# Splitting PSUM into two halves that change use separately, with early scores, VectorE weight factors and later means, in a two-layer attention kernel

## The chip, the cores and the metric

The kernel runs on one core of a Trainium2 chip. The metric is the device time of one execution in microseconds (us); each time quoted is the median of the runs of one submission. Every run of this study was in the fast state. Profiles are of one execution; their span is some 2 us shorter than the measured time. PE is TensorE, DVE is VectorE, ACT is ScalarE, POOL is GpSimd.

## The reference

Two attention layers over a batch of 8 images of 512 channels and 32 x 32 = 1024 positions, all in fp32. Each layer is:

```python
xn  = group_norm(x, 8 groups) * gamma + beta
q, k, v = Wq xn + bq, Wk xn + bk, Wv xn + bv      # 512x512 weights
attn = softmax(q k^T / 8)                          # 8 heads of 64 channels
x   = x + Wp (attn v) + bp
```

So there are 16 jobs (8 images, 2 layers). A job is a linear phase (k, the output projection of the job before, v, q) and an attention phase. The jobs of two images alternate, so that the normalisation of the next job runs during the attention of this one.

## The kernel before

**Linear phases.** Each 512x512 product is done by a Winograd-like scheme: seven products of half size instead of eight, on sums of the blocks of the input (`t`) and of the weights (`S1` to `S4`, the weight factors). A phase has two groups, i = 0 and 1. A group uses four PSUM banks, z, y, u, v:

```python
product(w, src, t, which, i, z, 1, True)      # needs xn only
note(1, z, s1)
product(w, src, t, which, i, y, 2, True)      # needs xn only
join(0, 0, y, s1)
product(w, src, t, which, i, z, 6, False)     # needs the 2nd sum, factor S2
note(2, z, s2)
product(w, src, t, which, i, u, 5, True)      # needs the 1st sum, factor S1
note(5, u, s5)
product(w, src, t, which, i, z, 7, False)     # needs the 3rd sum, factor S3
...                                           # notes and joins, products 3 and 4
```

A note reads PSUM (ACT for k and q), a join adds two parts into the result (DVE).

**Attention phases.** 64 items, each one block of 128 keys for one of 8 groups of queries. Item i does its scores on PE, the exponential on ACT, a running sum of the exponentials on DVE (`acc`; no sum at the first item of a group of eight), and two items later its values on PE. Every fourth item may carry a chore of the next job: statistics, means, scaling, sums.

**PSUM.** One pool of all eight banks, opened anew for each phase; the new pool waits for every user of the pool that it replaces.

```python
with tc.tile_pool(name=f"psa_{n}", bufs=2, space=PSUM) as pool:   # attention: 2 x 2 banks of scores, 2 x 2 of values
...
with tc.tile_pool(name=f"psl_{n}", bufs=2, space=PSUM) as pool:   # linear: z, y, u, v twice
```

The weight factors are made by POOL when weights arrive for the first time; the means (`group_mean`) take a score buffer at items 20 and 24, or at 4 and 8 where the statistics were done earlier.

## Time and profile before

| | before |
|---|---|
| time | 3440.8 us (3437.1 to 3443.2, 4 runs) |
| profile span | 3437.2 us |
| PE busy | 3340.0 us |
| DVE busy | 2318.8 us |
| ACT busy | 1379.5 us |
| POOL busy | 65.6 us |

Busy counts the time in which an engine executes something. The lines that say what bounds the kernel, and where PE loses time, are in the prediction; most of it is lost at the seams, the changes from one phase to the next.

### The profile page before, as it was taken

The numbers are of one execution on the slowest core, as the hardware profiler recorded it, in microseconds if no ns is written. First come the engines' busy times: TensorE is split into PE (matmuls) and PEld (weight loads), VectorE is DVE, ScalarE is ACT, GpSimd is POOL, SyncE is SP. The second block draws the span as 40 slices with busy tenths as digits, with TensorE's granted clock in tenths as the row PEclk, the third lists the DMA queues.
The fourth block names the chain that finished last, engine by engine and source line by source line (L and its number), as shares of the span: only waits on it lengthen the run. The fifth ranks groups of instructions, "written<-read, shape, count | busy, mean of one in ns | idle before, by whom it ended". The sixth has DMA issues, their size and how long they took to land.

```text
span 3437.2 us, 50762 instructions
## 1 busy us (share of the span) xinstructions
PE 3340.0 (97%) x20996; PEld 1487.2 (43%) x20996; DVE 2318.8 (67%) x3160; ACT 1379.5 (40%) x1535; POOL 65.6 (2%) x58
## 2 busy tenths in 40 slices
PE   7999999999999999999999999999999999999999
PEld 4335353353533535344353443534435354353533
DVE  4775948659386584865839668485683956748566
ACT  1532616335163351623516245162451625416153
POOL 3001000000000000000000000000000000000000
PEclk9999999999999999999999999999999999999999
DMA  5011010120201100021010010002101001000101
GB/s 190 14 48 71 22 37 15 54 77 22 73 15 35 47 24 22 15 70 61 23 71 18 32 50 21 22 18 81 51 21 71 18 32 50 21 22 21 44 11 43
DMA packets 79534, 141.81 MB, mean 41 GB/s; under 512 B 37568, under 2 KB 45760, under 8 KB 75200
## 3 DMA queue, kind: packets, MB, share of 16 engines
q1 hardware_dynamic: 79296, 138.50, 11.7%
q8 instruction: 166, 2.72, 0.3%
q14 instruction: 72, 0.59, 0.1%
HBM read 104.35 MB, written 31.98 MB: 40 GB/s over the span
## 4 chain that ended last, share of the span: by engine, by line
PE 86%; DVE 10%; issue 2%; ACT 2%; DMA 0%; SPq 0%; DVEq 0%; POOL 0%; ACTq 0%; POOLq 0%
PE sc L426 21%; PE po L449 19%; PE z L264 14%; PE u L264 9%; DVE acc L437 5%; PE z L257 5%; PE y L264 5%; PE v L264 5%; PE u L257 3%; ACT e L431 2%; PE y L257 2%; PE v L257 2%; PE pp L398 1%; DVE q L469 1%; DVE acc L435 1%
## 5 line engine op out<-in xcount | busy, mean ns | idle before, releaser
L431 ACT ACTIVATE e<-sc 128x1024 f32<-128x1024 f32 x1024 | 1046.5, 1024 | 674.7 <-PE sc L426 613.4
L426 PE MATMUL sc<-q,k 64*64 64x512 f32 x8192 | 1063.8, 591 | 34.7 <-DVE q L309 14.0
L449 PE MATMUL po<-e,v 64*64 64x512 f32 x8192 | 1057.3, 589 | 0.0
L437 DVE TENSOR_TENSOR acc<-acc,e 128x1024 f32<-128x1024 f32 x768 | 938.3, 1222 | 76.5 <-ACT e L431 25.1
L426 PEld LDWEIGHTS sc<-q,k 64*64 64x64 f32 x8192 | 307.8, 133 | 597.3 <-issue 540.6
L449 PEld LDWEIGHTS po<-e,v 64*64 64x64 f32 x8192 | 313.3, 133 | 565.6 <-issue 554.3
L264 PE MATMUL z<-xn,w 128*128 128x512 f32 x512 | 248.9, 610 | 41.4 <-DVE q L469 35.7
L305 ACT ACTIVATE sa<-z,vec_sb 128x512 f32<-128x512 f32 x128 | 88.0, 687 | 487.9 <-PE z L264 487.9
L435 DVE TENSOR_TENSOR acc<-e,e 128x1024 f32<-128x1024 f32 x128 | 156.4, 1222 | 137.4 <-ACT e L431 136.3
L264 PEld LDWEIGHTS z<-xn,w 128*128 128x128 f32 x512 | 97.0, 192 | 164.0 <-issue 107.3
L459 DVE TRANSPOSE_TENSOR_REDUCE r<-acc 128x32 f32<-128x1024 f32 x128 | 158.5, 1238 | 0.6
L362 ACT ACTIVATE sb<-z,vec_sb 128x512 f32<-128x512 f32 x30 | 20.6, 687 | 340.9 <-PE z L264 340.9
L334 ACT COPY sb<-u 128x512 f32<-128x512 f32 x32 | 18.8, 586 | 337.5 <-PE u L257 337.5
L264 PE MATMUL y<-xn,w 128*128 128x512 f32 x256 | 124.9, 611 | 0.0
L264 PE MATMUL z<-t,w 128*128 128x512 f32 x256 | 122.0, 599 | 2.1 <-DVE t L239 2.1
L257 PE MATMUL z<-w,xn 128*128 128x256 f32 x512 | 121.0, 379 | 0.0
L264 PE MATMUL u<-t,w 128*128 128x512 f32 x256 | 120.4, 592 | 0.0
L264 PE MATMUL u<-xn,w 128*128 128x512 f32 x256 | 120.3, 592 | 0.0
L264 PE MATMUL v<-t,w 128*128 128x512 f32 x256 | 120.3, 592 | 0.0
L309 DVE TENSOR_TENSOR q<-sb 128x512 f32<-128x512 f32 x32 | 22.4, 700 | 142.1 <-ACT sb L305 142.1
L264 PE MATMUL z<-q,w 128*128 128x512 f32 x240 | 112.8, 592 | 0.0
L257 PEld LDWEIGHTS z<-w,xn 128*128 128x128 f32 x512 | 97.3, 190 | 20.1 <-issue 7.7
(106 smaller groups left out, 2731.3 us busy)
## 6 DMA issues: line engine op xcount, KB each, us to landing
w<-keep SPq DMA_DIRECT2D x24, 1792.0 KB, 7.2
rb<-rd SPq DMA_DIRECT2D x256, 128.0 KB, 2.9
x<-x_dram SPq DMA_DIRECT2D x32, 512.0 KB, 5.8
out_dram<-x SPq DMA_DIRECT2D x64, 256.0 KB, 2.0
keep<-w SPq DMA_DIRECT2D x8, 1792.0 KB, 5.7
lr<-r SPq DMA_DIRECT2D x512, 4.0 KB, 1.7
w<-wqkv_dram SPq DMA_DIRECT2D x24, 256.0 KB, 5.2
w<-wp_dram SPq DMA_DIRECT2D x8, 256.0 KB, 5.9
```

What stands on the lines that cost most here:

```text
L257: nc.tensor.matmul(ps[:, ti * CH : (ti + 1) * CH], block[:, cc, t0 : t0 + P], w[:, slot, cc, :], start=(first and ti == 0 and cc == 0), st ...
L264: nc.tensor.matmul(ps, w[:, slot, cc, i * P : (i + 1) * P], block[:, cc, :], start=(first and cc == 0), stop=(cc == 1), skip_group_check=True,
L305: nc.scalar.activation(out, ps, AF.Identity, bias=env.vec(layer, bias, oc))
L309: nc.vector.tensor_add(dst[:, 2 * oh + i, cols], a, b)
L398: nc.tensor.matmul(ps, w[:, cc, oc * P : (oc + 1) * P], qt[0][:, cc, cols], start=(cc == 0), stop=(cc == NC - 1),)
L426: nc.tensor.matmul(sc[h * HD : (h + 1) * HD, j, :], k[r, hp, k0 : k0 + HD], q[r, hp, sh * HALF : (sh + 1) * HALF], start=True, stop=True,)
L431: nc.scalar.activation(e, sc, AF.Exp, scale=SCALE)
L435: nc.vector.tensor_add(acc[g], es[i - 1], e)
L437: nc.vector.tensor_add(acc[g], acc[g], e)
L449: nc.tensor.matmul(po[g][j * HD : (j + 1) * HD, h, :], v[r, kc, d0 : d0 + HD], e[r, j, :], start=(kc == 0), stop=(kc == NT - 1),)
L459: nc.vector.tensor_reduce(r, a.rearrange("p j (b e) -> p (j b) e", e=RP), AX.X, ALU.add, apply_transpose=True,)
L469: nc.vector.tensor_add(q[:, hp, cols], p[:, 1, :], px)
```

## The change

Its intent: keep PE busy over the seams between phases. PSUM becomes two halves (scores or z, y, u, v of group 0 in one; values or group 1 in the other), each turned over when its own users are done. The first two scores of an attention phase are issued inside the last q products. The weight factors go to DVE. The means move to items 24 and 32, and what follows them later too. Cut to its core:

```diff
-        with tc.tile_pool(name=f"psa_{n}", bufs=2, space=PSUM) as pool:
-        with tc.tile_pool(name=f"psl_{n}", bufs=2, space=PSUM) as pool:
+    def banks(half, use):
+        if half in ps:
+            ps.pop(half)[0].__exit__(None, None, None)
+        turns[0] += 1
+        guard = tc.tile_pool(
+            name=f"ps{half}_{turns[0]}", bufs=2 if use == "two" else 1, space=PSUM,
+            side=("left", "right")[half], reuse_waits="tile",
+        )
+        ps[half] = (guard, guard.__enter__())
 ...
-        nc.gpsimd.tensor_add(w[:, S1], w[:, S3], w[:, A22])      # and three more
+        def factor(part):                                        # called later, piece by piece
+            if part == 0:
+                nc.vector.tensor_add(w[:, S1], w[:, S3], w[:, A22])
 ...
         product(w, src, t, which, i, y, 2, True)
         join(0, 0, y, s1)
+        yield                          # the first k phase runs two groups side by side
         product(w, src, t, which, i, z, 6, False)
 ...
         join(1, 1, s3, s5)
+        if break_in is not None:
+            break_in()                 # scores 0 and 1, in q's second group
         product(w, src, t, which, i, u, 3, False)
 ...
+        if together:                   # first k phase only
+            b = channel_group(n, K, BK, kt[0], 1)
+            next(a)
+            next(b)
+            for step in together:      # sums of xn, factors of k
+                step()
+            run(a)
+            run(b)
 ...
-            chores = reads + steps                               # one at each fourth item
+            chores = dict(zip((4, 8, 12, 16), reads))
+            chores.update(zip((24, 32, 36, 40, 44, 48, 52), steps))
+            chores.update({56: t[0], 60: t[1]})
```

A thing that the title of the change doesn't say: the new pools are also opened with `reuse_waits="tile"`. A tile then waits only for the last users of its own banks, not for all users of the pool that lay there.

More of the change, by code (lines that the diff above doesn't have):

```diff
@@ L1 @@
-from contextlib import ExitStack, contextmanager
+from contextlib import ExitStack
 import concourse.bass as bass
@@ L82, in fast_path @@
     wdram = ctx.enter_context(tc.tile_pool(name="wdram", bufs=1, space=DRAM))
-    ps = {}
+    ps, turns = {}, [0]
     bv_sb = [acts.tile([P, C], F32, name=f"bv_sb{i}") for i in range(2)]
@@ L104, in advance, with bank @@
             t[1]()
-    @contextmanager
-    def attention_banks(n):
-        with tc.tile_pool(name=f"psa_{n}", bufs=2, space=PSUM) as pool:
-            ps["pool"] = pool
-            yield
-    @contextmanager
-    def linear_banks(n):
-        with tc.tile_pool(name=f"psl_{n}", bufs=2, space=PSUM) as pool:
-            ps["pool"] = pool
-            yield
+    def banks(half, use):
[7 more added lines that the diff above has]
+        ps[half] = (guard, guard.__enter__())
     def two_banks(tag, name):
-        return ps["pool"].tile([P, 2, HALF], F32, tag=tag, name=name)
-    def bank(tag, name):
-        return ps["pool"].tile([P, HALF], F32, tag=tag, name=name)
+        return ps[0 if tag == "sc" else 1][1].tile([P, 2, HALF], F32, tag=tag, name=name)
+    def bank(half, tag, name):
+        return ps[half][1].tile([P, HALF], F32, tag=tag, name=name)
     weights = {}
@@ L139, in fetch @@
         if weights.get(which, (None, None))[0] == layer:
-            return
-        w = wpool.tile([P, NW, 2, CH], F32, tag=f"w{which}", name=f"w_{which}_{layer}_{len(stored)}_{clock[0]:.0f}")
+            return None
+        turns[0] += 1
+        w = wpool.tile([P, NW, 2, CH], F32, tag=f"w{which}", name=f"w_{which}_{turns[0]}")
         weights[which] = (layer, w)
@@ L144, in fetch, with factor_later @@
             nc.sync.dma_start(w, stored[which, layer])
-            return
+            return None
         for at, i, j in ((A11, 0, 0), (A12, 0, 1), (A22, 1, 1), (S3, 1, 0)):
             nc.sync.dma_start(w[:, at], raw_block(layer, which, i, j))
-        nc.gpsimd.tensor_add(w[:, S1], w[:, S3], w[:, A22])
-        nc.gpsimd.tensor_sub(w[:, S2], w[:, S1], w[:, A11])
-        nc.gpsimd.tensor_sub(w[:, S3], w[:, A11], w[:, S3])
-        nc.gpsimd.tensor_sub(w[:, S4], w[:, A12], w[:, S2])
         keep = wdram.tile([P, NW, 2, CH], F32, name=f"keep_{which}_{layer}")
         stored[which, layer] = keep
-        later(60.0, lambda: nc.sync.dma_start(keep, w))
+        def factor(part):
+            if part == 0:
+                nc.vector.tensor_add(w[:, S1], w[:, S3], w[:, A22])
+            elif part == 1:
+                nc.vector.tensor_sub(w[:, S2], w[:, S1], w[:, A11])
+            elif part == 2:
+                nc.vector.tensor_sub(w[:, S3], w[:, A11], w[:, S3])
+            else:
+                nc.vector.tensor_sub(w[:, S4], w[:, A12], w[:, S2])
+                later(1.0, lambda: nc.sync.dma_start(keep, w))
+        return factor
+    def factor_later(delay, factor):
+        if factor is not None:
+            for part in range(4):
+                later(delay + 1.7 * part, lambda part=part: factor(part))
     def load_x(b):
@@ L181, in group_mean @@
             if alone:
-                pm = bank("z", name)
+                pm = bank(0, "z", name)
                 nc.tensor.matmul(pm[:, :NC], env.blk, src, start=True, stop=True)
@@ L229, in fast_path @@
     qt, kt, vt = [None], [None], [None]
-    background = []
     def combine(src, t, part):
@@ L245, in product @@
     def product(w, src, t, which, i, ps, p, first):
-        slot, block = {
-            1: (A11, src[:, 0:2, :HALF]), 2: (A12, src[:, 2:4, :HALF]),
-            3: (S4, src[:, 2:4, HALF:]), 4: (A22, t[:, 2]), 5: (S1, t[:, 0]),
-            6: (S2, t[:, 1]), 7: (S3, src[:, 0:2, HALF:]),
-        }[p]
+        slot = (A11, A12, S4, A22, S1, S2, S3)[p - 1]
+        if p in (4, 5, 6):
+            block = t[0][:, {5: 0, 6: 1, 4: 2}[p]]
+        else:
+            rows = 0 if p in (1, 7) else 2
+            cols = slice(0, HALF) if p in (1, 2) else slice(HALF, S)
+            block = src[:, rows : rows + 2, cols]
         if which == V:
@@ L268, in product, with seven @@
         advance(1.72)
-    def seven(n, which, src, t, i, note, join):
+    def seven(n, which, src, t, i, note, join, break_in=None):
         w = weights[which][1]
         tag = f"{which}_{n}_{i}"
-        z, y = bank("z", f"z{tag}"), bank("y", f"y{tag}")
-        u, v = bank("u", f"u{tag}"), bank("v", f"v{tag}")
+        z, y, u, v = (bank(i, f"{b}", f"{b}{tag}") for b in "zyuv")
         sa = epool.tile([P, 2, HALF], F32, tag="e", name=f"sa{tag}")
@@ L294, in seven @@
         join(1, 0, v, s3)
-    def channel_phase(n, which, bias, dst):
-        layer = jobs[n][1]
-        for i in range(2):
-            def note(k, ps, out):
-                if k == 5:
-                    nc.scalar.copy(out, ps)
-                else:
-                    oc = i if k < 3 else 2 + i
-                    nc.scalar.activation(out, ps, AF.Identity, bias=env.vec(layer, bias, oc))
-            def join(oh, sh, a, b):
-                cols = slice(sh * HALF, (sh + 1) * HALF)
-                nc.vector.tensor_add(dst[:, 2 * oh + i, cols], a, b)
-            seven(n, which, xn[0], tx[0], i, note, join)
-            if background:
-                background.pop(0)()
@@ L315, in k_phase, with run, channel_group, note @@
-    def k_phase(n):
-        kt[0] = acts.tile([P, NC, S], F32, tag="k", name=f"k_{n}")
-        channel_phase(n, K, BK, kt[0])
-    def q_phase(n):
-        qt[0] = acts.tile([P, NC, S], F32, tag="q", name=f"q_{n}")
-        channel_phase(n, Q, BQ, qt[0])
+    def run(*parts):
+        parts = list(parts)
+        while parts:
+            parts = [g for g in parts if next(g, g) is not g]
+    def channel_group(n, which, bias, dst, i, break_in=None):
+        layer = jobs[n][1]
+        def note(k, ps, out):
+            if k == 5:
+                nc.scalar.copy(out, ps)
+            else:
+                oc = i if k < 3 else 2 + i
+                nc.scalar.activation(out, ps, AF.Identity, bias=env.vec(layer, bias, oc))
+        def join(oh, sh, a, b):
+            cols = slice(sh * HALF, (sh + 1) * HALF)
+            nc.vector.tensor_add(dst[:, 2 * oh + i, cols], a, b)
+        return seven(n, which, xn[0], tx, i, note, join, break_in)
@@ new lines, in k_phase, with q_phase, first_scores @@
+    def k_phase(n, together=()):
+        kt[0] = acts.tile([P, NC, S], F32, tag="k", name=f"k_{n}")
+        a = channel_group(n, K, BK, kt[0], 0)
+        if together:
[6 more added lines that the diff above has]
+            run(b)
+        else:
+            run(a)
+            banks(1, "one")
+            run(channel_group(n, K, BK, kt[0], 1))
+    def q_phase(n, reads):
+        qt[0] = acts.tile([P, NC, S], F32, tag="q", name=f"q_{n}")
+        run(channel_group(n, Q, BQ, qt[0], 0))
+        for step in reads:
+            step()
+        banks(0, "two")
+        att = Attention(n)
+        def first_scores():
+            att.scores(0)
+            att.scores(1)
+        run(channel_group(n, Q, BQ, qt[0], 1, first_scores))
+        banks(1, "two")
+        return att
@@ L346, in join @@
                 )
-            seven(n, V, xn[0], tx[0], i, note, join)
+            run(seven(n, V, xn[0], tx, i, note, join))
     def proj_phase(n):
@@ L375, in join, with plain_weights @@
                     nc.sync.dma_start(out[b, oc * P : (oc + 1) * P, cols], at(oh, sh))
-            seven(n, O, qt[0], to[0], i, note, join)
+            run(seven(n, O, qt[0], to, i, note, join))
         if layer == 1 and b + 2 < B:
             load_x(b + 2)
-    def last_proj(n):
-        b, layer = jobs[n]
-        xt = xs[b]
+    def plain_weights(n):
+        layer = jobs[n][1]
         w = wpool.tile([P, NC, C], F32, tag=f"w{K}", name="w_last")
@@ L387, in last_proj, with plain_proj @@
         return w
-    def last_proj_run(n, w):
+    def plain_proj(n, w):
         b, layer = jobs[n]
         xt = xs[b]
-        tags = "zyuv"
         for sh in range(2):
@@ L395, in last_proj_run @@
             for oc in range(NC):
-                ps = bank(tags[oc], f"pp_{n}_{sh}_{oc}")
+                ps = bank(sh, "zyuv"[oc], f"pp_{n}_{sh}_{oc}")
                 for cc in range(NC):
@@ L406, in last_proj_run, with __init__, scores @@
                 advance(3.5)
-    def attention(n, chores):
-        q, k, v = qt[0], kt[0], vt[0]
-        last = n + 1 == len(jobs)
-        if last:
-            groups = [(hp, sh) for sh in range(2) for hp in range(HP)]
-        else:
-            groups = [(hp, sh) for hp in range(HP) for sh in range(2)]
-        steps = [(g, kc) for g in range(len(groups)) for kc in range(NT)]
-        es, acc, po = {}, {}, {}
-        def scores(i):
+    class Attention:
+        def __init__(self, n):
+            self.n, self.q, self.k, self.v = n, qt[0], kt[0], vt[0]
+            if n + 1 == len(jobs):
+                self.groups = [(hp, sh) for sh in range(2) for hp in range(HP)]
+            else:
+                self.groups = [(hp, sh) for hp in range(HP) for sh in range(2)]
+            self.steps = [(g, kc) for g in range(len(self.groups)) for kc in range(NT)]
+            self.es, self.acc, self.po = {}, {}, {}
+        def scores(self, i):
+            n, q, k = self.n, self.q, self.k
+            groups, steps, es, acc = self.groups, self.steps, self.es, self.acc
             g, kc = steps[i]
@@ L437, in scores, with values @@
                 nc.vector.tensor_add(acc[g], acc[g], e)
-        def values(i):
+        def values(self, i):
+            n, v = self.n, self.v
+            groups, steps, es, po = self.groups, self.steps, self.es, self.po
             g, kc = steps[i]
@@ L452, in values, with finish @@
                     )
-        def finish(g):
+        def finish(self, g):
+            n, q = self.n, self.q
+            groups, acc, po = self.groups, self.acc, self.po
             hp, sh = groups[g]
@@ L493, in finish, with run @@
             later(11.5 if ends else 14.6, normalise)
-        for i in range(len(steps) + LEAD):
-            if i < len(steps):
-                scores(i)
-            if i >= LEAD:
-                values(i - LEAD)
+        def run(self, chores):
+            steps = self.steps
+            for i in range(2, len(steps) + LEAD):
+                if i < len(steps):
+                    self.scores(i)
+                self.values(i - LEAD)
                 g, kc = steps[i - LEAD]
                 if kc == NT - 1:
-                    finish(g)
+                    self.finish(g)
                     advance(0.85)
-            if chores and i >= 4 and i % 4 == 0:
-                chores.pop(0)()
-            advance(1.71)
-        assert not chores
+                if i in chores:
+                    chores[i]()
+                advance(1.71)
     def judge():
@@ L527, in fresh_to, with fetch_bv, sums, start @@
         to[0] = acts.tile([P, 3, 2, HALF], F32, tag="v", name=f"to_{n}")
+    def fetch_bv(layer):
+        nc.sync.dma_start(bv_sb[layer], bv[layer : layer + 1, :].to_broadcast([P, C]))
+    def sums(n):
+        def start():
+            tx[0] = acts.tile([P, 3, 2, HALF], F32, tag="t", name=f"t_{n}")
+            combine(xn[0], tx[0], 0)
+        return [start] + [lambda part=part: combine(xn[0], tx[0], part) for part in (1, 2, 3)]
+    def out_sums(n, src):
+        def start():
+            to[0] = acts.tile([P, 3, 2, HALF], F32, tag="v", name=f"to_{n}")
+            combine(src, to[0], 0)
+        later(12.6, start)
+        for part in range(1, 4):
+            later(12.6 + part * 1.7, lambda part=part: combine(src, to[0], part))
+    banks(0, "one")
+    banks(1, "one")
     load_x(0)
-    fetch(K, 0)
-    fetch(V, 0)
+    factor_k = fetch(K, 0)
+    factor_v = fetch(V, 0)
     fetch_bv(0)
-    fetch(Q, 0)
+    factor_q = fetch(Q, 0)
     load_x(1)
-    fetch(O, 0)
+    factor_o = fetch(O, 0)
     fetch_bv(1)
-    with linear_banks(0):
-        reads, steps = norm_steps(0, alone=True)
-        for step in reads + steps:
-            step()
-        fresh_t(0)
-        for part in range(4):
-            combine(xn[0], tx[0], part)
-        k_phase(0)
-        v_phase(0)
-        q_phase(0)
+    reads, steps = norm_steps(0, alone=True)
+    for step in reads + steps:
+        step()
+    t = sums(0)
+    k_phase(0, [
+        t[0], t[1], lambda: factor_k(0), lambda: factor_k(1), t[2], lambda: factor_k(2),
+        lambda: factor_k(3), t[3], lambda: factor_later(1.0, factor_v),
+    ])
+    factor_later(1.0, factor_q)
+    v_phase(0)
+    factor_later(1.0, factor_o)
+    att = q_phase(0, [])
     reads, steps = norm_steps(1)
@@ L549, in fast_path @@
         last = n + 1 == len(jobs)
+        chores = {}
         if last:
-            w = last_proj(n)
-            chores = []
-        else:
-            chores = reads + steps
-            chores += [lambda: (fresh_t(n + 1), combine(xn[0], tx[0], 0))]
-            chores += [lambda: combine(xn[0], tx[0], 1)]
-        with attention_banks(n):
-            attention(n, chores)
-        with linear_banks(n + 1):
-            if last:
-                advance(100.0)
-                advance(100.0)
-                judge()
-                last_proj_run(n, w)
-                continue
-            src = qt[0]
-            combine(xn[0], tx[0], 2)
-            combine(xn[0], tx[0], 3)
-            later(12.6, lambda: (fresh_to(n), combine(src, to[0], 0)))
-            for part in range(1, 4):
-                later(12.6 + part * 1.7, lambda part=part: combine(src, to[0], part))
-            k_phase(n + 1)
-            layer2 = jobs[n + 2][1] if n + 2 < len(jobs) else None
-            if layer2 is not None:
-                fetch(K, layer2)
-            proj_phase(n)
-            if n + 2 < len(jobs):
-                fetch(O, jobs[n + 1][1])
-            v_phase(n + 1)
-            if layer2 is not None:
-                fetch(V, layer2)
-                reads, steps = norm_steps(n + 2)
-                if layer2 == 1:
-                    background.append(lambda r=tuple(reads): [f() for f in r])
-                    reads = []
-            q_phase(n + 1)
-            if layer2 is not None:
-                fetch(Q, layer2)
@@ new lines, in fast_path @@
+            w = plain_weights(n)
+        else:
+            t = sums(n + 1)
+            chores = dict(zip((4, 8, 12, 16), reads))
+            chores.update(zip((24, 32, 36, 40, 44, 48, 52), steps))
+            chores.update({56: t[0], 60: t[1]})
+        att.run(chores)
+        banks(0, "one")
+        if last:
+            banks(1, "one")
+            advance(100.0)
+            advance(100.0)
+            judge()
+            plain_proj(n, w)
+            break
+        t[2]()
+        t[3]()
@@ new lines, in fast_path @@
+        out_sums(n, qt[0])
+        ahead = n + 2 < len(jobs)
+        k_phase(n + 1)
+        if ahead:
+            factor_later(8.0, fetch(K, jobs[n + 2][1]))
+        proj_phase(n)
+        if ahead:
+            factor_later(8.0, fetch(O, jobs[n + 1][1]))
+        v_phase(n + 1)
+        reads = steps = []
+        if ahead:
+            factor_later(8.0, fetch(V, jobs[n + 2][1]))
+            reads, steps = norm_steps(n + 2)
+        early = ahead and jobs[n + 2][1] == 1
+        att = q_phase(n + 1, reads if early else [])
@@ L591, in general_path @@
+        if early:
+            reads = []
+        if ahead:
+            factor_later(125.0, fetch(Q, jobs[n + 2][1]))
+    for half in (1, 0):
+        ps.pop(half)[0].__exit__(None, None, None)
 @with_exitstack
```

## The prediction

> **What bounds the kernel now.** I read the page first, for the engine that sets the time.
>
> ```profile
> PE 3340.0 (97%) x20996; PEld 1487.2 (43%) x20996; DVE 2318.8 (67%) x3160; ACT 1379.5 (40%) x1535; POOL 65.6 (2%) x58
> ...
> PEclk9999999999999999999999999999999999999999
> ```
>
> TensorE is busy for 3340.0 of 3437.2 us. No scheduling change can shorten those; it can win back only the 97 us of idle, and slow matmuls. So the second view was the waits of PE alone (who released it, us in total, times, longest):
>
> ```profile
> PE z L264 <- DVE q L469: 35.7, 15, 2.7
> PE sc L426 <- DVE q L309: 14.0, 16, 0.9
> PE sc L426 <- ACT e L431: 11.8, 46, 0.3
> PE pm L183 <- DVE mv L178: 10.6, 1, 10.6
> PE sc L426 <- DVE mean L193: 8.9, 8, 1.2
> PE z L264 <- ACT xn L213: 5.7, 1, 5.7
> PE pp L398 <- DVE q L469: 2.4, 1, 2.4
> PE z L264 <- DVE t L239: 2.1, 1, 2.1
> ```
>
> The counts name the places: 15 and 16 are the seams between the 16 attention and 16 linear phases, 8 is one item in two, 1 is the start or the end. A "busy" PE need not run at peak, so the third view was the timeline of PE at one seam of each kind (start, duration, engine, line, count, idle before):
>
> ```profile
> 634.08 2.75 PE L449 MATMUL po<-e,v 64*64 64x512 f32 x24
> 639.19 1.98 PE L264 MATMUL z<-xn,w 128*128 128x512 f32 x4 [2.35 <-DVE q L469]
> 641.01 1.88 PE L264 MATMUL y<-xn,w 128*128 128x512 f32 x4
> ...
> 733.85 1.88 PE L264 MATMUL v<-t,w 128*128 128x512 f32 x4
> 736.60 1.95 PE L426 MATMUL sc<-q,k 64*64 64x512 f32 x16 [0.88 <-DVE q L309]
> 738.88 1.09 PE L426 MATMUL sc<-q,k 64*64 64x512 f32 x8 [0.32 <-ACT e L431]
> 739.78 1.04 PE L449 MATMUL po<-e,v 64*64 64x512 f32 x8
> 740.64 1.04 PE L426 MATMUL sc<-q,k 64*64 64x512 f32 x8
> ```
>
> In steady state a product (four matmuls) starts every 1.717 us (0.429 each, against a shown duration of 0.592, whose tail overlaps the next one), and an attention step of 16 quarter-array matmuls also takes 1.717. The last values are six rounds of four at once, so the next matmul could start at 634.08 + 6 x 0.429 = 636.65; the first seam loses 639.19 - 636.65 = 2.54 us, and another 0.10 in its first weight load. At the second the first score should start at 733.85 + 1.717 = 735.57, and the fourth at 739.00 after three scores and one value group of 0.86 each; it starts at 740.64, so 1.64 us are lost.
>
> A fourth view, the first linear products after an attention phase, shows a loss that no wait counts:
>
> ```profile
> 213.80 3.01 PE L264 MATMUL z<-xn,w 128*128 128x512 f32 x4 [2.35 <-DVE q L469]
> ...
> 216.60 2.59 PE L264 MATMUL y<-xn,w 128*128 128x512 f32 x4
> ```
>
> From 213.80 the first two products take 5.23 us until the third starts, against 3.54 after 639.19. Five of the 15 seams and the last projection look so: weight loads follow each other by 0.85 us, half speed. About 1.6 us each.
>
> [...] The kernel before changes mode only across waits, so its trace can't show the cost; [...] the 128x1024 sum of xn at 22.08 us took 2.29 us beside GpSimd's factors and 1.22 elsewhere, and so did their GpSimd partner (1.26 alone, 2.24 beside it).
>
> **The change, part by part.** The work on PE stays the same.
>
> Attention to linear. Before, the linear pool could not open until the whole attention pool was read, the last reader being the final add of the values (L469). Now k's first group uses the half of the scores, free since the last exponential (210.0 in job 0, before PE ends its values at 211.3). Its first two products need nothing new. The third and fourth need sums made in attention; the fifth needs the third sum, due 6.9 us into the phase, while VectorE made it 4.1 us after PE ended its values; moving the first two sums to items 56 and 60 adds perhaps 1 us of backlog, still in time. Saved: 16 x 2.54 (15 seams and the last projection) [...]: 38.1 us.
>
> Linear to attention. The first two scores run inside the last q products, in the half that group 0 of q has left. Their exponentials take 2 x 1.02 us on ACT under two products of 1.72, so the third score and the first values find all they need. Saved 16 x 1.64 = 26.2; but three mode changes per seam (to quarter, back, to quarter: 0.21 + 0.27 + 0.21 = 0.69) cost 11.0. Net 15.2 us.
>
> Half-speed products: with no idle, six times 1.6 us go: 9.6.
>
> Means at items 24 and 32. In attention VectorE is nearly full: per group of 8 steps (13.7 us) seven sums of 1.22, a reduction 1.25, the value add 0.65, the inversion 1.2, the scaling 0.67 come to 12.3, and with the statistics (5.9) it lags. The score buffer taken by the mean is given back late:
>
> ```profile
> 775.15 1.09 PE L426 MATMUL sc<-q,k 64*64 64x512 f32 x8 [1.19 <-DVE mean L193]
> ```
>
> At an item whose step has no sum (24 and 32 start groups) VectorE reaches the copy a sum of 1.22 us sooner, and has had four more steps to catch up. I take 8 of the 8.9 us.
>
> Start. [...]
>
> ```profile
> 14.04 1.22 DVE L205 TENSOR_TENSOR mul<-var,vec_sb 128x4 f32<-128x4 f32 x1 [1.20 <-POOL var L201]
> 15.29 6.87 DVE L207 TENSOR_SCALAR xn<-x,mean,mul 128x1024 f32<-128x1024 f32 x4
> ...
> 18.36 3.78 PE L264 MATMUL z<-xn,w 128*128 128x512 f32 x4 [5.72 <-ACT xn L213]
> ```
>
> The small multiply would take 0.16 and the first scaling 0.81 (the mean later is 0.81, here 1.72), so PE starts about 2.0 us sooner. The interleaving of the two k groups gives four products that need no sums, which covers the 2.1 us wait for t. From 18.36 to 98.33 the 42 products (72.3) lost 7.7 us; about 1 of that is the seam, 2.1 the wait, most of the rest half speed[...]: 2 more. Start: 6 us.
>
> GpSimd beside later phases: the second attention phase has sums of 1.74 and 2.10 us instead of 1.22, with about 1 us lost on PE. Saved: 1. Against it, 32 factor operations of 0.69 us (22 us, from the 128x512 adds) go to VectorE, mostly in linear phases, where it is busy 40 to 47 of 97 us: beside PE. But VectorE is in order: a factor that waits for its weights (four transfers, 5.2 us to landing, issued after the phase's last product; the factor is placed some 8.6 us later) holds the v and proj evictions that PE needs next. For three such phases I charge 2 us.
>
> Sum: 38.1 + 15.2 + 9.6 + 8 + 6 + 1 - 2 = 75.9, so 3440.8 - 75.9 = 3365. From below: 658 products of 1.717, 224 v products of 1.727, 1024 steps of 1.717, 64 last matmuls of 0.429 and 15 x 0.93 us of means are 3316; with 16.4 before the first product, 2.8 of half speed, 13.6 of mode changes, 5.2 after PE's last and about 2.5 between profile span and measured time: 3357, with nothing for small waits. I say 3362.
>
> **The rivals.** (a) Mode changes cost more [...] At 0.5 us each instead of 0.24 the 64 of them take 16 us more: 3378, within 2%. (b) VectorE becomes the bound at the seams: it is busy 104 of 116 us in an attention phase with statistics, and now PE no longer pauses to let it catch up 4 us per item. Against it: ACT, not VectorE, feeds k and q, and the exponentials wait for VectorE only 0.7 us at most now. If k's fifth product waited 2 us at each seam, 30 us would go back: 3393. (c) The whole gain arrives and mode changes hide in the pipeline: 3349. (d) The idle of a seam was only a buffer wait over a true one, so that it comes back under another name: against it, every operand of the first products is ready at 211. I give it little.
>
> **Range and chances.** 2% is 3372. The centre, 3362, is 10 us under it; (a) and a mild (b) lie across the line, (c) on the far side. Range 3348 to 3382. Faster by over 2%: 0.75; within 2%: 0.23; slower: 0.02, for nothing adds work to PE but mode changes.
>
> **What would show it.** The waits of PE on q L469 and on the last q add gone, and the mean's wait at most 1 us in all; PE idle below 35 us; a period of 207 to 209 us from item to item (211.45 at best before); the first matmuls after a seam at 0.43 spacing, those of a mode change later by about 0.2; the first product near 16.4. Wrong if mode changes leave 0.5 us holes, if k's fifth product waits on the sum of xn, or if v and proj products wait on VectorE behind a factor.

How it priced the mode changes: the 0.21 and 0.27 us in its sum of 0.69 are the author's estimate from the trace of the kernel before. The shown duration of a matmul exceeds the spacing by 0.592 - 0.429 = 0.16 us, and the first loads after idle cost 0.05 (quarter tiles) or 0.10 us (full ones). The 38.1 us for the first seam are 16 x 2.54 less 16 x 0.16.

## The result, and the profile after

The changed kernel takes 3362.4 us (3361.3 to 3363.9, 4 runs) against 3440.8: 78 us less. The ratio is 0.977 (95% interval 0.976 to 0.979). Ratios here are the mean time of one kernel's fast runs over that of the other's of the same rounds, so not quite the ratio of the medians quoted.

The same two lines of the page, now of the changed kernel:

```profile
PE 3328.4 (99%) x20996; PEld 1483.2 (44%) x20996; DVE 2319.4 (69%) x3192; ACT 1378.3 (41%) x1535; POOL 16.9 (1%) x26
...
PEclk9999999999999999999999999999999999999999
```

PE has the same 20996 matmuls; its idle time went from 97.2 to 32.3 us (3360.7 - 3328.4). The waits of PE alone:

```profile
PE pm L195 <- DVE mv L190: 11.2, 1, 11.2
PE sc L470 <- ACT e L475: 6.6, 30, 0.2
PE z L277 <- DVE w L155: 4.7, 1, 4.7
PE z L277 <- ACT xn L225: 3.6, 1, 3.6
PE pvar L195 <- DVE dev L208: 0.8, 1, 0.8
```

The groups with counts of 15 and 16, the seams, are gone, and so are the waits on the mean. What is left is the start, and 30 short waits at the means. One line is new: 4.7 us on a weight factor (`w`). The two seams, in PE's timeline of the changed kernel (a mode change is PE's switch between matmuls on the whole 128x128 array and four 64x64 ones at once):

```profile
207.40 2.76 PE L495 MATMUL po<-e,v 64*64 64x512 f32 x24
210.09 1.98 PE L277 MATMUL z<-xn,w 128*128 128x512 f32 x4
...
93.43 1.88 PE L277 MATMUL z<-xn,w 128*128 128x512 f32 x4
95.24 1.95 PE L470 MATMUL sc<-q,k 64*64 64x512 f32 x16
97.11 1.98 PE L277 MATMUL u<-xn,w 128*128 128x512 f32 x4
98.94 1.88 PE L277 MATMUL v<-t,w 128*128 128x512 f32 x4
100.75 1.09 PE L470 MATMUL sc<-q,k 64*64 64x512 f32 x8
```

From attention to linear: the six rounds of values end their slots at 207.40 + 2.57 = 209.97, and k starts at 210.09; 0.11 us are lost where 2.54 were, besides the 0.10 in the first loads that both kernels have. From linear to attention, 93.43 plus three products and two scores' worth twice (4 x 1.717) gives 100.30 for the third score; it starts at 100.75 and its own first loads cost 0.05: 0.50 us lost where 1.64 were. From job to job (the prediction says from item to item) the period is now 207.9 us, once 208.2 (in the chain of work, the last values of successive phases start at 207.58, 415.47, 623.36 and so on), where it was 211.5 to 215. At all 64 mode changes after the start the first load begins together with the first matmul, where most tiles in steady state have theirs 0.43 us ahead.

Now the start, in the timeline of DVE and PE together:

```profile
24.46 1.88 PE L277 MATMUL y<-xn,w 128*128 128x512 f32 x4
26.44 0.69 DVE L330 TENSOR_TENSOR k<-y,sa 128x512 f32<-128x512 f32 x1 [2.74 <-PE y L277]
27.05 1.22 DVE L248 TENSOR_TENSOR t<-xn 128x1024 f32<-128x1024 f32 x1
...
31.00 3.75 PE L277 MATMUL z<-t,w 128*128 128x512 f32 x4 [4.67 <-DVE w L155]
```

DVE stands idle for 2.74 us until PE has finished the fourth product, only to add two parts of k (the join), and makes the sum `t` after that. PE then waits 4.7 us for the sums and factors and runs its next products at half speed (a duration of 3.75 for four matmuls instead of 1.88; the mean granted clock is 0.62 from 31.00 to 36.64), and the gain of the start is lost: the last q product before attention would, without the scores between, start at 98.94 - 2.08 = 96.86 us (2.08 = two scores 1.72 and one pair of mode changes 0.36), against 95.58 in the kernel before. About 0.6 of these 1.3 us is scatter: PE's first matmul, which waits for the statistics of the first image, came at 11.20 in this execution and at 10.64 in that of the kernel before.

### The profile page after: what moved, and what is told of

Its sections match the earlier page's. It is cut to its first block, busy times and chain, and to the rows that moved or that the text cites. A ratio compares the mean times of both kernels' runs of the same rounds, so it can differ in the third digit from the quotient of the medians.

```text
span 3360.7 us, 50799 instructions
## 1 busy us (share of the span) xinstructions
PE 3328.4 (99%) x20996; PEld 1483.2 (44%) x20996; DVE 2319.4 (69%) x3192; ACT 1378.3 (41%) x1535; POOL 16.9 (1%) x26
## 4 chain that ended last, share of the span: by engine, by line
PE 97%; ACT 1%; DVE 1%; DMA 0%; issue 0%; SPq 0%; POOL 0%; DVEq 0%; POOLq 0%
PE sc L470 26%; PE po L495 25%; PE z L277 15%; PE u L277 10%; PE z L270 5%; PE y L277 5%; PE v L277 5%; PE u L270 3%; PE y L270 2%; PE v L270 2%; ACT e L475 1%; PE pp L440 1%; DVE acc L481 0%; DMA x<-x_dram 0%; DVE stats L189 0%
## 5 line engine op out<-in xcount | busy, mean ns | idle before, releaser
L537 DVE TENSOR_TENSOR q<-q,rb 128x512 f32<-128x512 f32 x128 | 86.6, 677 | 40.8 <-DMA rb<-rd 40.8
```

What stands on the lines that cost most here:

```text
L537: nc.vector.tensor_mul(q[:, hp, cols], q[:, hp, cols], rb)
```

## The experiments

The theory after reading the two traces: the seams give the gain, by freeing banks earlier; the place of the means gives some 10 us; the start loses about 7 us to the order of work in DVE's queue. What was open: whether the halves, the finer waits or the early scores win the seams, what a mode change costs, whether the means' gain comes from "later" or from the place, and what the factors' move is worth. Twelve kernels ran; all gave correct results. They ran in four submissions, and the kernel before ran again in each: its medians were 3439.5 to 3440.9 us, so that differences of 2 or 3 us between submissions are known to about 1 us.

**1. Sums first at the start.** In the first k phase the joins move behind the sums and factors in DVE's queue:

```diff
         product(w, src, t, which, i, y, 2, True)
-        join(0, 0, y, s1)
         yield
+        join(0, 0, y, s1)
```

> The changed kernel with one edit: in the first k phase VectorE makes the sums of xn and k's weight factors before the two joins of k, not after them. Theory: the changed kernel lost its gain at the start because the joins, which wait for TensorE's second and fourth product (at 22.7 and 26.2 us), stand ahead of the sums in VectorE's queue, so the fifth product waited 4.7 us (31.0 instead of 26.2) and then ran at half speed. With the edit PE has no wait between its first product (16.8 us) and the first attention phase, the fifth product starts at about 26.2 us, the eighth-in-line full-speed start at 36.6 moves to about 29.6, and the span falls by 7 us (3360.7 to about 3354; ratio to before 0.975). Rival: the sums wait for the scaling and shifting of xn or for the weights' transfers, and the fifth product starts no sooner than 29 us; the span falls by less than 3 us.

Measured: 3355.1 us (ratio 0.975), 7.4 us less than the changed kernel; span 3352.4. The first product began at 16.29 (0.55 of that gain is the scatter of the statistics again), and the fifth product no longer waits; DVE's second factor is done 3.2 us before:

```profile
21.25 0.69 DVE L155 TENSOR_TENSOR w<-w 128x512 f32<-128x512 f32 x1
...
25.16 1.88 PE L277 MATMUL z<-t,w 128*128 128x512 f32 x4
```

The theory holds: an order of instructions, not any data, cost 7 us.

**2. k in the other half.** k's first group takes the half that the values leave last, its second the half of the scores:

```diff
-        a = channel_group(n, K, BK, kt[0], 0)
+        a = channel_group(n, K, BK, kt[0], 0, None, 0 if together else 1)   # its half
 ...
-            banks(1, "one")
-            run(channel_group(n, K, BK, kt[0], 1))
+            banks(0, "one")
+            run(channel_group(n, K, BK, kt[0], 1, None, 0))
 ...
-        banks(0, "one")                                  # after attention
+        banks(1, "one")
```

> The changed kernel with k's first group put in the half of PSUM that the values' sums leave last, and its second in the half of the scores; everything else in two halves as now. Theory: the first k product waits again for the last add of the values. That add now ends 6.2 us after the last round of values starts (213.59 - 207.40; before 5.05), so the wait is 3.5 us at 15 seams, 52 us, plus half speed at some of the seams or all (1.6 us each, 8 to 24 us): span 3420 to 3437, the gain of the change mostly gone. Rival: a wait behind the buffer would have come anyway and little (under 15 us) changes.

Measured: 3361.4 us (ratio 0.977), no change. The theory fell as stated. The halves were not what freed k: within the values' half, z and y fall on the buffer of the group of queries before the last one, which has long been read, and the pool's finer waits see that. So the halves and the finer waits had to be told apart:

**3 and 4. Finer waits alone, and halves alone.** The kernel before with `reuse_waits="tile"` added to its two pools and nothing else; and the changed kernel with `reuse_waits="tile"` taken out:

```diff
-        with tc.tile_pool(name=f"psa_{n}", bufs=2, space=PSUM) as pool:
+        with tc.tile_pool(name=f"psa_{n}", bufs=2, space=PSUM, reuse_waits="tile") as pool:
 ...                                                      # and psl_ likewise
```

> The kernel before with one edit: its two alternating pools of all eight banks stay, but a tile that lands on banks of the pool that was closed waits only for the last users of its own banks, as the changed kernel's pools do, and not for every user of the closed pool. No halves, no early scores, factors on GpSimd, means as before. It asks whether the halves or the finer waits win the seams, after the run with k in the other half moved nothing. Theory (finer waits): at the first seam z, y and u fall on banks of the scores and of the values' free buffer, so the 2.54 us less 0.11 for the mode change go 16 times (39 us) and six half-speed stretches (9.6 us); at the second the last add of q is not waited for, 0.88 us become 0.09, 16 times (13 us); the third score's 0.6 us and the means' 8.9 us stay. Span 3437 - 61 = 3376, time about 3380. Rival (the halves are needed): within 10 us of before.

> The changed kernel with its halves, but each pool waits for all users of the pool that lay there. Theory: the halves alone also suffice, since k's first group and the first two scores fall on a half that is long free; only the first values of a phase must wait for the last add of q in their half (due about 0.1 us after they are now issued) and v's later groups change nothing, so 0 to 3 us are lost: 3362 to 3366. Rival: the halves do nothing without the finer waits, and 40 us or more come back.

Measured: the finer waits alone 3374.5 us (ratio 0.981), the halves alone 3362.5 (ratio 0.977, as the changed kernel). In the first, the seam is closed by the words in the pool alone:

```profile
208.02 2.75 PE L449 MATMUL po<-e,v 64*64 64x512 f32 x24
210.71 1.98 PE L264 MATMUL z<-xn,w 128*128 128x512 f32 x4
```

210.71 is again 0.11 us after the end of the slot at 208.02 + 2.57. The finer waits alone gave 65 us, where I expected 60. Either suffices for this seam; the change has both.

**5. Neither.** k in the other half and pools that wait for all users:

> Both taken away at the first seam: k's first group in the values' half and pools that wait for all users of the one before. Theory: now k's first product does wait for the last add of the values, about 3.5 us at 15 seams (52 us), and half of the seams or more then run 1.6 us slow: span 3415 to 3437. If it moves nothing either, the add was never what k waited for.

Measured: 3433.9 us (20 runs, 3430.1 to 3439.1; ratio 0.998): the whole gain of the change gone. The wait is the one named, in PE's list and in the timeline of the first seam:

```profile
PE z L277 <- DVE q L518: 53.4, 15, 4.1
...
214.28 3.78 PE L277 MATMUL z<-xn,w 128*128 128x512 f32 x4 [3.50 <-DVE q L518]
```

The duration of 3.78 is half speed: the next product starts 3.58 us later, at 217.86, where 1.717 is the steady period. In the chain of work, ten of the 15 seams begin with such slow products, with gaps of 3.6 us in the mean of all 15 (53.4 / 15) and 4.1 at most; in the kernel before, with 2.4 us in the mean (35.7 / 15), it was five. So the gap between the values' last add and k was a wait for a buffer and for nothing else.

**6. No early scores.** The two scores after the last q product:

```diff
-        run(channel_group(n, Q, BQ, qt[0], 1, first_scores))
+        run(channel_group(n, Q, BQ, qt[0], 1))
+        first_scores()
```

> The changed kernel with the first two scores issued after the last q product instead of between its products. Theory: most of the 1.64 us per seam came back through the two halves (the scores no longer wait for the last add of q, 0.9 us and its restart), and only a wait of the third score on the first exponential (0.6 us by the trace of before) is what the break-in itself removes, while it costs two more mode changes that the trace shows at 0.09 to 0.2 us each. So without it the seam loses about 0.7 us where it now loses 0.5: span +3 us, up to 3364. Rival: the break-in is what wins the seam; without it 1.3 us per seam or more come back: +20 us, 3381.

Measured: 3364.9 us (ratio 0.978), 2.5 us slower than the changed kernel. What comes back is the third score's wait on the first exponential (PE's list: 46 waits of 12.0 us instead of 30 of 6.6); the period from job to job is 208.10 instead of 207.89. The theory holds: of the 18 us won at this seam, the early scores won 2 or 3.

**7. Early scores apart.** One score before each of the last two q products, so two more mode changes per seam:

> The changed kernel with the two early scores apart: one before the last but one q product, one before the last. That adds two mode changes per seam, 32 in all, and no other work; it measures what a mode change costs. Theory (0.09 to the quarter array with 0.05 in its first loads, 0.10 back with 0.11): 0.36 us per seam more, 5.7 us in all, span 3366. My prediction's estimate (0.48 per pair): 7.7 us, 3368. Rival (a change costs 0.5 us, hidden here by something): 16 us.

Measured: 3367.1 us (ratio 0.979), 4.6 us more. The first product of that execution began 0.7 us sooner than in the changed kernel's (the statistics were done at 10.5 instead of 11.2), so the 16 extra pairs cost about 5.3 us, 0.33 each. In the timeline they cost 0.36, and the period from job to job, which has no start in it, is 0.36 longer too (208.25 instead of 207.89):

```profile
94.43 1.09 PE L473 MATMUL sc<-q,k 64*64 64x512 f32 x8
95.45 1.98 PE L277 MATMUL u<-xn,w 128*128 128x512 f32 x4
97.37 1.09 PE L473 MATMUL sc<-q,k 64*64 64x512 f32 x8
```

From 94.43 to 95.45 are 1.02 us for 0.86 of scores, from 95.45 to 97.37 1.92 for a product of 1.717. That is 0.09 to the quarter array and 0.05 in its first loads, 0.11 back and 0.11 in the first loads. The estimate of 0.48 was a third too high; the rival of 0.5 per change is out.

**8 and 9. The place of the means.** At items 20 and 24 as before (with the scalings, and the sums at 48 and 52, back where they were), and at 23 and 31:

```diff
-            chores.update(zip((24, 32, 36, 40, 44, 48, 52), steps))
+            chores.update(zip((20, 24, 28, 32, 36, 40, 44), steps))      # run 8
+            chores.update(zip((23, 31, 36, 40, 44, 48, 52), steps))      # run 9
```

> The changed kernel with the means at items 20 and 24 and what follows them four to eight items sooner, as in the kernel before. Theory: the score that takes the mean's buffer next waits 1.2 us or a little more at the 8 or so items whose statistics lie in attention, since VectorE no longer has a pause at the seams: +9 to +13 us, 3371 to 3375, with the wait on the mean back in PE's list. Rival (the waits came from the pauses and are gone with them): +0 to +3.

> The changed kernel with the two means at items 23 and 31 instead of 24 and 32, everything else where it is. Between 20 and 24 both the time that VectorE has to catch up and the place in the group change: item 24 starts a group and has no sum, item 23 ends one and has one of 1.22 us that stands ahead of the mean's copy. Theory (the place counts): at 23 the slack falls by 1.22 us; about 0.5 to 1 us is waited for at some 8 to 15 first means, +4 to +12 us, 3366 to 3374. Rival (only being later counts): within 2 us of 3362.

Measured: 3377.9 us (ratio 0.982) and 3383.8 us (ratio 0.983): 15.5 and 21.4 us more than the changed kernel, both more than I expected. PE's waits, first of the run at 20 and 24, then of the run at 23 and 31:

```profile
PE sc L470 <- DVE mean L205: 12.6, 15, 1.2
```

```profile
PE sc L470 <- DVE mean L205: 9.2, 15, 1.7
...
PE sc L470 <- DVE var L212: 6.0, 15, 0.7
```

Each place waits at 15 jobs, not 8: in these runs every job has its means there, where the kernel before had half of them at items 4 and 8. And the list is short of the truth: the shown end of a matmul lies 0.16 us after the next one could start (0.592 shown, 0.429 apart), so by that overlap each listed wait costs 0.16 more: 12.6 + 15 x 0.16 = 15.0, and 9.2 + 6.0 + 30 x 0.16 = 20.0, near the measured 15.5 and 21.4. (By the period from job to job the surplus is 0.23 a wait in these two runs: 209.31 or 208.64 us at item 20, for listed waits of 1.19 or 0.53, against 207.89. The slower first loads after idle, 0.05, are part of the rest.) Per job the first mean waits 0.84 us at item 20 (12.6 / 15), 0.61 at 23 and nothing listed at 24; the second waits nothing at 24 and 32, and 0.40 at 31 (6.0 / 15), though that is seven items later than 24. These means mix two kinds of job. Where the statistics run in attention too, the first mean waits 1.19 us at item 20 and 0.90 at 23 (more at two of seven); elsewhere it waits 0.53 and 0.22. So three items of catching up are worth 0.3 us, and the last item, which opens a group and so has no sum of 1.22 us ahead of the mean's copy, takes away all that is left, up to 0.9. The place is the larger cause; "later" as such helps a little. That run 9 is the slower one comes from having both means at a bad place, where run 8 has one.

**10. Factors on GpSimd.** Run 1 with the weight factors back on POOL:

> The run with the sums first at the start, but with the weight factors on GpSimd, started as soon as the weights land, as in the kernel before. It prices the move of the factors to VectorE. Theory: at the start [...] the scaling of xn takes 6.9 us instead of 3.0 and the first product comes 2 us later; the second attention phase again loses about 1 us: +3 to +4 us on 3355, 3358 to 3359. Rival: VectorE's 22 us of factors cost as much as they save, so that GpSimd's version is equal or faster.

Measured: 3357.6 us (ratio 0.976), 2.6 us more than run 1. The scaling takes 6.87 us instead of 2.98 and the first product begins at 18.52 instead of 16.29:

```profile
15.46 6.87 DVE L217 TENSOR_SCALAR xn<-x,mean,mul 128x1024 f32<-128x1024 f32 x4
```

and in run 1:

```profile
14.23 2.98 DVE L219 TENSOR_SCALAR xn<-x,mean,mul 128x1024 f32<-128x1024 f32 x4
```

The second attention phase, where about 1 us more was expected, shows no wait of PE. So the move of the factors is worth 2.6 us, 2.2 of them before the first product; as the change was built, the order of the joins hid it.

**11. A faster version.** Run 1, and at the item after each mean the values before the scores on PE:

```diff
+                swap = i - 1 in chores and i - 1 in (24, 32)
-                if i < len(steps):
+                if i < len(steps) and not swap:
                     self.scores(i)
                 self.values(i - LEAD)
+                if swap:
+                    self.scores(i)
```

> A version meant to beat both: sums first at the start, and at the item after each mean the values go before the scores on PE. The changed kernel waits 0.22 us at each of 30 means for the exponential that still reads the score buffer, because the mean has taken the other one (6.6 us in PE's list). With values first the buffer is free in time, and the mean's copy, which ends 1.5 us after the mean at the latest in the items looked at, is still done before the score after next needs its buffer 1.96 us later. Theory: those 6.6 us go: 3355 - 6.6 = 3348. Rival: the score after next, which now comes 0.27 us sooner after the mean, waits for the copy and takes the gain back: 3354 or more.

Measured: 3347.0 us (3345.7 to 3347.2, 5 runs; ratio 0.973). The 30 waits on the exponential are gone from PE's list; four short ones on the mean's copies took their place, 0.7 and 0.6 us in all:

```profile
PE sc L470 <- DVE mean L205: 0.7, 2, 0.5
...
PE sc L470 <- DVE var L212: 0.6, 2, 0.3
```

The gain of 8 us is over the listed 6.6, but below what 0.16 more for each wait would give (6.6 + 4.8, less 1.9 for the four new ones: 9.5). The period from job to job, 207.25 in most jobs instead of 207.89, says 0.32 for each wait of 0.22, so here the surplus was 0.10. Why it differs from that of runs 8 and 9 is open.

**12. Finer waits and the means' place, nothing else.** The kernel before with the edit of run 3 and the chores' items of the changed kernel:

> The kernel before with two edits only: the finer waits for its pools, and the means at items 24 and 32 with the scalings and sums placed as in the changed kernel. No halves, no early scores, factors on GpSimd. Theory (the gains add up): the run with the finer waits alone took 3374.5 us and still waited 9.5 us in eight places on the mean, each 0.16 us dearer than the list says (the shown end of a matmul lies 0.16 us after the next one could start), so 10 to 11 us go: 3364, within 3 us of the full change; early scores (2.5 us), the factors' move (2.6 us once the start is in order) and the lost start make up the rest. Rival: without the halves the later means run into the end of attention (sums at 56 and 60, then k's fifth product waits), and 3 us or less is gained.

Measured: 3362.9 us (3362.6 to 3364.5, 5 runs; ratio 0.978), equal to the whole change. So the means' place brings about 12 us on top of the 65 of the finer waits, and the rest of the change, halves, early scores, factors and the interleaved first k phase, comes to nothing in sum: early scores about +2.5, the start -1.3, and little else.

## Why the prediction was right

The time (3362.4 against 3362) and the direction were right, and the mechanism at the seams was the named one. The closeness is in part luck: the largest error and the smaller ones cancelled. By its own steps, in us saved:

| step | predicted | measured | from |
|---|---|---|---|
| attention to linear | 38.1 | 38.9 | 16 x (2.54 - 0.11), traces |
| linear to attention | 15.2 | 18.2 | 16 x (1.64 - 0.50), traces |
| half-speed products | 9.6 | 10.1 | five seams with 5.23 instead of 3.54 for two products, last projection 29.37 instead of 27.73; none left after the start |
| means | 8 | about 10 | 8.9 + 8 x 0.16; run 12 against run 3: 11.6 |
| start | 6 | -1.3 | 95.58 - 96.86, of it 0.6 scatter; run 1 gives 7.4 back |
| GpSimd in later phases | 1 | at most 0.4 | 2.6 of run 10, less 2.2 at its start; a wait of 0.55 on the second phase's mean is counted above |
| factors that wait | -2 | 0 | no such wait in PE's list after the start |
| sum | 75.9 | about 76.3 | span 76.5, time 78.4 |

**The start was wrong.** The step that failed reads: "The interleaving of the two k groups gives four products that need no sums, which covers the 2.1 us wait for t." I looked at what the products need and not at what stands ahead of the sums in DVE's queue. The first two joins come before them in program order and wait for those four products, so the sums began after them, at 27.05 us (in run 1, with the joins behind them, at 17.31). The 2 us for half speed that ends earlier were the author's estimate; in run 1, where PE waits for nothing between its first product and attention, that product took 3.57 us to the next start and the second 1.87, where the kernel before has 3.57 from 18.36 and again 3.39 from 26.72, after its wait. The other half of that step was right: with no factors on GpSimd beside it the scaling took 0.75 us a piece (1.72 before) and the first product came at 16.84 (predicted 16.4).

**Mode changes** were estimated at 0.21 and 0.27 us; the trace shows 0.14 and 0.22. The rival of 0.5 us is refuted by run 7.

**The seams.** All that the prediction said of waits was seen: the wait on the values' last add and that on q's last add are gone, k's fifth product does not wait (it starts at 217.06, its sum was made from 214.11 to 215.3), and at the seams no wait came back under another name. But its reason was incomplete. At the first seam it credits the half of the scores; run 2 shows that k may as well lie in the other half, run 3 that no halves are needed, and run 4 that halves without the finer waits also suffice. At the second it puts the whole saving down to the early scores in the freed half; by run 6 issuing them early is worth 2.5 of the 18 us, and the freed banks the rest. The rival (d), a true wait behind the buffer's, is refuted by runs 3 and 4.

**The means.** The place was rightly named as the cause ("items 24 and 32 start groups"); "and has had four more steps to catch up" is the smaller part, 0.3 of the 0.53 or 1.19 us that a first mean waits at item 20. The size was low because a listed wait leaves out the 0.16 us or so by which the shown end of a matmul overlaps the next.

**The factors.** The charge of 2 us for waits behind a transfer was not needed: one factor waited 1.8 us for its weights, and PE did not wait for it.

The difference of about 2 us between the change in span and in measured medians is mostly the choice of the execution: the profiled one of the kernel before took 3439.1 us, 1.7 less than the median. What stays open is why a listed wait costs 0.10 us more in one run and 0.23 in others, and why after a gap of 2.4 us some seams are slow and others not.

For two measurements the runs show no mechanism. With longer gaps at equal work (run 5) ten of the 15 seams are slow, where it was five; in the two products after 213.80 of the kernel before the mean granted clock is 0.67, in those after 639.19 it is 1.00. And the scaling took 6.87 us with POOL's factors beside it (run 10), 2.98 without (run 1).

## What to carry to other kernels

When PE waits at the seam between two phases for the last reader of a buffer pool, first ask whether the next tile's own banks are free: a finer wait can be worth more than a new layout. Check not only what an operation needs but what stands ahead of it in its engine's queue; moving two small adds behind the sums was worth 7 us here. Put a borrowed buffer's release where the releasing engine has no long work queued before it, and count each listed wait of PE as 0.1 to 0.2 us dearer than the list says, if the matmuls' shown ends overlap as here.
